# Attention on one core: the shift products of two heads as 32-row tiles, and the products with v in runs over four blocks of keys

## The chip, the cores and the metric

The kernel runs on one core of one Trainium2 chip. Its time is the device time of one launch in microseconds (us); shown are medians over runs of the same program. Besides those runs there is one profiled execution, from which all views of the trace come.

## The reference, cut to what matters

The input is x of shape (8, 1024, 512) in float32. With `xn = layernorm(x)` the result is `x + attention(xn) + ffn(xn)`.

Attention has 16 heads of 32 columns:

```python
qkv = xn @ W_attn + b_attn            # (8, 1024, 1536), split into q, k, v
att = einsum('bhqd,bhkd->bhqk', q, k) * 32 ** -0.5
att = where(causal, att, -inf)
att = softmax(att, axis=-1)
y   = einsum('bhqk,bhkd->bhqd', att, v)
out = y @ W_proj + b_proj
```

The feed-forward part quantises its input, its three weight matrices and its hidden values in blocks of 16 to a four-bit grid, and computes `down(silu(gate(xn)) * up(xn))` with 1408 hidden columns. The change does not touch it, but its products share TensorE with attention.

## The kernel before

**Work units.** Tokens are handled in 64 tiles of 128. Attention is cut into 64 units, one for each of the 8 batches and each pair of heads (`HU = 2`). A unit goes through two passes. The first, `maxima` (L555), computes the scores with queries on the partitions (product L594), takes each row's maximum on VectorE (L608) and the sum of its exponentials on ScalarE (L566). It leaves, for every query and head, the negated maximum as two float32r parts, a high and a low one, and the inverse of the sum. The second, `weigh` (L668), computes the scores again with keys on the partitions, and is what the change edits.

**The second pass.** A unit's queries come in two halves `Q` of 512 columns (`W`). For each half the loop over `j` (L704) runs over the blocks of 128 keys that the half may look at: four for the first half, eight for the second. In the half's own four blocks the columns before the block's first query are left out (`q0`), so products there are 512, 384, 256 and 128 columns wide; elsewhere they are 512 wide. For each block and each of the two heads there are two products into one PSUM bank:

- the **shift product** (L710) puts the negated maximum of each query into all 128 partitions. Its moving operand is `shT`, a tile of 128 rows in which four strips of 32 rows belong to the four pairs of half and head; only the first two rows of a strip hold anything (the high and the low part), and the others are zero. Its stationary operand `pick[:, k, :]` has ones in the 32 rows of strip `k` and zeros elsewhere, so that all 128 rows are run through though one strip counts;
- the **score product** (L713) adds keys times queries. Its 128 rows are the four combinations of high and low parts of q and k, 32 rows each.

Both are float32r and stand in the trace as one matmul record each. ScalarE then writes the exponential into an SBUF tile `pr` (L721; a pool of eight buffers), and for the blocks on the diagonal GpSimd clears the triangle (L727). The **products with v** (`weighted`, L688 to L701) take these tiles: stationary are 32 columns of `vs`, moving is `pr`, and the 32 output rows go to one of four strips of the bank `y`, by head and by whether the block is even or odd; `tile_position=(0, row)` names that strip, so that four such products can run in TensorE at once, each in 32 columns of the array. They are float32, which the trace shows as two matmul records for each product. Before the change, two blocks (four products) are done in one run.

**What sets the order.** The order of the instructions on every engine is written by the program itself. Each part of the work is a generator that yields the estimated cost of what it has just emitted, the time on the plan's clock before which it should not go on, and the number of PSUM banks that it wants. `merge` (L994) picks whose turn it is, among six streams: `weigh`, `maxima`, the feed-forward network, the quantisation, the preparation of later tiles, and `finish`. So numbers such as the `cost` in L722 are planned costs; they decide what is emitted between what, and nothing else. Loads and stores go out on SyncE's queue at planned times (`Later`). All products but those with v use the six shared banks of `Banks` (L185); `y` and the accumulator of the down projection `acc` (L793) have a bank each.

Other lines that the text speaks of: L349 transposes, L464 and L509 the projections to q, k and v, L641 the transpose of the maxima, L815 the gate and up products and L793 the down product of the network, L920 the output projection.

Of the kernel before, what the change touches and what calls it, by code (L numbers as in the profile page):

```python
# [27 lines left out]
def kernel(  # L28
# [35 lines left out]
    HD = D // HEADS  # L64
# [6 lines left out]
    HU = 2  # L71
    NU = HEADS // HU
    assert NU == NT
    QG = 4
    W = QG * P
# [38 lines left out]
    pick = const.tile([P, HPC, P], F32R, name="pick")  # L114
# [33 lines left out]
    def act(columns, after=0.0, function="other"):  # L148
        if function == "other":
            function = table[0]  # L150
        switch = TABLE if function != table[0] else 0.0
        table[0] = function
        return on("act", 0.17 + 0.00083 * columns + switch, after)
# [4 lines left out]
    def pool(us, after=0.0):  # L158
        return on("pool", us, after)
# [52 lines left out]
    banks = Banks()  # L212
# [320 lines left out]
    def load_half(un, h):  # L533
        f, r0 = un.u * HU // HPC, un.u * HU % HPC
        for name, pool, s, pieces, lst in (("qs", p5, 0, (0, 0, 1, 1), un.qs), ("ks", p6, 1, (0, 1, 0, 1), un.ks)):
            tl = pool.tile([P, HU, W], F32R, name=name)
            for g, piece in enumerate(pieces):
                nc.sync.dma_start(
                    out=tl.bitcast(F32)[g * HD : (g + 1) * HD],
                    in_=un.batch.qk[s, piece, f, r0 * HD : (r0 + HU) * HD, h * W : (h + 1) * W].rearrange(  # L540
                        "(r d) t -> d r t", d=HD
                    ),
                )
            lst.append(tl)

    def load_values(un):
        for h in range(2):
            v = p4.tile([P, QG, HU * HD], F32, name="vs")
            cols = slice(un.u * HU * HD, (un.u + 1) * HU * HD)
            nc.sync.dma_start(  # L550
                out=v, in_=un.batch.v[h * QG : (h + 1) * QG, :, cols].rearrange("t p e -> p t e")
            )
            un.vs.append(v)
# [114 lines left out]
    def weigh(un):  # L668
        f, r0 = un.u * HU // HPC, un.u * HU % HPC
        emptied = 0.0  # L670
        while un.shT is None:
            yield 0.0, clock[0] + 0.5, 0
        units_begun[0] = un.n

        def loads(Q):
            if un.n + 2 < N:
                load_half(units[un.n + 2], Q)
            if un.n + 1 < N and Q == 0:
                load_values(units[un.n + 1])

        yield 0.0, un.ready, 2

        for Q in range(2):
            Later(1.0, lambda Q=Q: loads(Q))
            y = ps_a.tile([P, W], F32, name="y")
            last = (Q + 1) * QG - 1
            waiting = []
            def weighted():  # L688
                for j, r, pr, q0 in waiting:
                    h, jj = j // QG, j % QG  # L690
                    row = (j % 2 * HU + r) * HD
                    nc.tensor.matmul(  # L692
                        y[row : row + HD, q0:],
                        lhsT=un.vs[h][:, jj, r * HD : (r + 1) * HD],
                        rhs=pr[:, q0:],
                        start=(j < 2),
                        stop=(j >= last - 1),
                        skip_group_check=True,
                        tile_position=(0, row),
                    )  # L700
                return 0.3 + (W - min(q0 for _, _, _, q0 in waiting)) * 0.0017  # L701

            ready = 0.0
            for j in range(last + 1):  # L704
                h, jj = j // QG, j % QG
                q0 = jj * P if h == Q else 0
                fresh = []
                for r in range(HU):
                    bank, w = banks.take()
                    nc.tensor.matmul(  # L710
                        w[:, q0:], lhsT=pick[:, Q * HU + r, :], rhs=un.shT[:, q0:], start=True, stop=False
                    )
                    nc.tensor.matmul(  # L713
                        w[:, q0:],
                        lhsT=un.ks[h][:, r, jj * P : (jj + 1) * P],
                        rhs=un.qs[Q][:, r, q0:],
                        start=False,
                        stop=True,
                    )
                    pr = p8.tile([P, W], F32, name="pr")  # L720
                    nc.scalar.activation(pr[:, q0:], w[:, q0:], AF.Exp)  # L721
                    cost = max(0.22, (W - q0) * 0.00089)  # L722
                    end = act(W - q0, clock[0] + cost * (r + 1), "exp")
                    banks.back(bank, end)
                    if h == Q:

                        nc.gpsimd.affine_select(  # L727
                            out=pr[:, q0 : q0 + P],
                            in_=pr[:, q0 : q0 + P],
                            compare_op=ALU.is_ge,  # L730
                            fill=0.0,
                            base=0,
                            pattern=[[1, P]],
                            channel_multiplier=-1,
                        )
                        end = pool(0.37, end)
                    if j == 1 and q0 > 0:

                        nc.gpsimd.memset(pr[:, :q0], 0.0)
                        end = pool(0.2)  # L740
                    fresh.append((j, r, pr, 0 if j < 2 else q0))
                if j % 2 == 0 and waiting:
                    yield 2 * cost, max(ready, emptied), 0
                    yield weighted(), 0.0, 2
                    waiting = []
                else:
                    yield 2 * cost, 0.0, 2 if j < last else 0
                waiting += fresh
                ready = end
            yield 0.0, max(ready, emptied), 0  # L750
            cost = weighted()
            yu = p1.tile([P, W], F32, name="yu")
            nc.scalar.copy(yu, y)
            emptied = act(W, clock[0] + cost)

            def store(Q=Q, yu=yu):
                rows = slice(r0 * HD, (r0 + HU) * HD)
                for part in range(2):
                    nc.sync.dma_start(
                        out=un.batch.y[part, f, rows, Q * W : (Q + 1) * W],  # L760
                        in_=yu[part * HU * HD : (part + 1) * HU * HD, :],
                    )
                un.batch.units_done += Q

            Later(emptied - clock[0] + 0.5, store)
            yield cost, 0.0, 2
# [275 lines left out]
    with tc.manual_schedule(  # L1042
# [10 lines left out]
        for k in range(2 * NC):  # L1053
            w = p8.tile([P, NC, P], F32, name="pr")
# [9 lines left out]
        for col in range(2 * D, 3 * D, 2 * P):  # L1064
            w = p2.tile([P, NC, 2 * P], F32, name="wa")
# [48 lines left out]
        def preparations():  # L1114
            for n in range(AHEAD, N, QT):
# [3 lines left out]
        merge(  # L1119
            [  # L1120
                Stream((weigh(un), 17.5, un.n, 1.0) for un in units),
                Stream((maxima(un), 6.0, un.n - 1 - SOONER, 1.0) for un in units[1:]),
                Stream(networks()),
# [43 lines left out]
```

## Time and profile before

| what | value |
|---|---|
| median of 3 runs (lowest, highest) | 4314.11 us (4312.82, 4318.57) |
| the profiled execution's own time | 4316.67 us |
| its span, first to last instruction | 4315.0 us |
| mean granted TensorE clock | 0.990 of full speed |
| ScalarE busy | 2331.1 us (54%) |
| VectorE busy | 2946.8 us (68%) |
| GpSimd busy | 551.6 us (13%) |
| shift products L710, 1536 records | 643.7 us busy, mean 427 ns |
| score products L713, 1536 records | 519.4 us busy, mean 346 ns |
| products with v L692, 3072 records | 358.1 us busy, mean 509 ns |

In the profile PE is TensorE's matmuls and PEld its weight loads, DVE is VectorE, ACT ScalarE, POOL GpSimd and SP SyncE. A matmul's recorded end is modelled, and matmuls of one group overlap in the record; the time that a product takes on TensorE is therefore read from the starts of neighbours, not from its own duration. The time outside the span is 4316.67 - 4315.0 = 1.67 us.

### The profile page before, as it was taken

How to read it: one execution, taken by the hardware profiler on the slowest of the kernel's cores; microseconds unless marked ns; L12 is line 12 of the kernel's file. 1: busy time of each engine (PE TensorE's matmuls, PEld its weight loads, DVE VectorE, ACT ScalarE, POOL GpSimd, SP SyncE). 2: the span in 40 equal slices, each digit the busy share in tenths (PEclk: the TensorE clock that was granted, in tenths of full speed). 3: DMA queues.
4: the chain of work that ended last, by engine and by line, in shares of the span. 5: the costliest groups of instructions: out<-in, count | busy, mean ns of one | idle time of the engine just before them, and what ended most of it. 6: DMA issues, size and time to landing. Idle time of an engine off the chain costs nothing.

```text
span 4315.0 us, 58501 instructions
## 1 busy us (share of the span) xinstructions
PE 4186.5 (97%) x17684; PEld 2574.7 (60%) x17684; DVE 2946.8 (68%) x6811; ACT 2331.1 (54%) x5918; POOL 551.6 (13%) x1295
## 2 busy tenths in 40 slices
PE   7779999999999999999999999999999999999998
PEld 6655556566666666666666666666666555555555
DVE  6786666666666766666766666766666677777755
ACT  2246565655555555555555555555555566666640
POOL 0001111111111111111111111111111111111110
PEclk9889999999999999999999999999999999999999
DMA  5654343454545554555554555554554433433424
GB/s 183 176 165 118 106 118 111 125 153 139 148 141 144 153 159 139 149 140 145 152 159 137 150 140 143 154 160 135 152 138 125 120 84 91 102 85 94 103 57 124
DMA packets 564185, 573.83 MB, mean 133 GB/s; under 512 B 114976, under 2 KB 420128, under 8 KB 563872
## 3 DMA queue, kind: packets, MB, share of 16 engines
q1 hardware_dynamic: 563872, 570.10, 47.8%
q8 instruction: 142, 2.33, 0.2%
q14 instruction: 171, 1.40, 0.1%
HBM read 400.56 MB, written 169.35 MB: 132 GB/s over the span
## 4 chain that ended last, share of the span: by engine, by line
PE 83%; DMA 3%; ACT 2%; DVE 2%; issue 1%; SPq 1%; ACTq 0%; POOL 0%; DVEq 0%
PE bank L815 26%; PE acc L793 13%; PE y L692 7%; PE bank L464 7%; PE bank L710 7%; PE bank L713 6%; PE bank L594 5%; PE bank L920 5%; PE bank L509 4%; PE bank L349 2%; ACT bank L566 2%; DVE neg L608 1%; DMA yT<-y_kept 1%; DMA ks<-y_kept 1%; DMA vs<-v_kept 0%
## 5 line engine op out<-in xcount | busy, mean ns | idle before, releaser
L608 DVE TENSOR_REDUCE neg<-bank 128x1 f32<-128x512 f32 (+3 forms) x1280 | 805.6, 635 | 292.3 <-PE bank L594 265.7
L721 ACT ACTIVATE pr<-bank 128x512 f32<-128x512 f32 (+3 forms) x1536 | 666.9, 494 | 517.5 <-PE bank L713 508.5
L566 ACT ACTIVATE bank<-bank,neg 128x512 f32<-128x512 f32 (+3 forms) x1536 | 857.9, 560 | 113.5 <-DVE neg L608 101.5
L727 POOL TENSOR_SCALAR_AFFINE_SELECT pr<-pr 128x128 f32<-128x128 f32 x1024 | 395.3, 397 | 3145.9 <-ACT pr L721 3139.2
L815 PE MATMUL bank<-wuT,xqT 128*128 128x512 f32 (+1 forms) x1536 | 674.7, 564 | 9.0 <-ACT bank L566 6.5
L815 PE MATMUL bank<-wgT,xqT 128*128 128x512 f32 (+1 forms) x1536 | 671.5, 561 | 0.0
L793 PE MATMUL acc<-wdT,hqT 128*128 128x512 f32 x1408 | 662.9, 595 | 1.3 <-ACT hqT L350 1.3
L594 PE MATMUL bank<-ks,qs 128*128 128x512 f32 (+3 forms) x1536 | 631.1, 469 | 20.1 <-ACT bank L566 14.5
L710 PE MATMUL bank<-shT,pick 128*128 128x512 f32 (+3 forms) x1536 | 643.7, 427 | 5.2 <-DMA shT<-shift_kept 3.6
L713 PE MATMUL bank<-qs,ks 128*128 128x512 f32 (+3 forms) x1536 | 519.4, 346 | 0.0
L606 DVE TENSOR_TENSOR bank<-bank,mask 128x128 f32<-128x128 f32 (+1 forms) x768 | 259.5, 338 | 342.6 <-PE bank L594 253.8
L594 PEld LDWEIGHTS bank<-ks,qs 128*128 128x128 f32 x1536 | 273.2, 191 | 266.4 <-issue 132.6
L476 ACT ACTIVATE full<-bank,bqk 128x256 f32<-128x256 f32 x256 | 107.5, 471 | 572.0 <-PE bank L464 503.6
L710 PEld LDWEIGHTS bank<-shT,pick 128*128 128x128 f32 x1536 | 290.8, 189 | 201.0 <-issue 94.1
L815 PEld LDWEIGHTS bank<-wuT,xqT 128*128 128x128 f32 x1536 | 273.8, 190 | 218.3 <-issue 140.6
L815 PEld LDWEIGHTS bank<-wgT,xqT 128*128 128x128 f32 x1536 | 276.0, 190 | 213.0 <-issue 164.8
L793 PEld LDWEIGHTS acc<-wdT,hqT 128*128 128x128 f32 x1408 | 258.3, 190 | 224.4 <-issue 204.1
L692 PE MATMUL y<-pr,vs 128*32 128x512 f32 (+3 forms) x3072 | 358.1, 509 | 4.7 <-POOL pr L727 4.6
L464 PE MATMUL bank<-xnT,wa 128*128 128x256 f32 x1536 | 352.2, 383 | 0.5 <-ACT xnT L350 0.5
L713 PEld LDWEIGHTS bank<-qs,ks 128*128 128x128 f32 x1536 | 291.2, 190 | 84.4 <-issue 51.9
L464 PEld LDWEIGHTS bank<-xnT,wa 128*128 128x128 f32 x1536 | 292.2, 192 | 64.8 <-issue 27.5
L566 ACT ACTIVATION_READ_ACCUMULATOR bank<-bank,neg 128x1 f32 x1536 | 316.0, 206 | 0.0
(97 smaller groups left out, 4501.5 us busy)
## 6 DMA issues: line engine op xcount, KB each, us to landing
wa<-in_L_attn_W_attn_dram SPq DMA_DIRECT2D x146, 512.0 KB
qs<-qk_kept SPq DMA_DIRECT2D x512, 128.0 KB
ks<-qk_kept SPq DMA_DIRECT2D x512, 128.0 KB
wp<-in_L_attn_W_proj_dram SPq DMA_DIRECT2D x81, 512.0 KB
qk_kept<-high SPq DMA_DIRECT2D x128, 256.0 KB
qk_kept<-full SPq DMA_DIRECT2D x128, 256.0 KB
y_kept<-yu SPq DMA_DIRECT2D x256, 128.0 KB
yT<-y_kept SPq DMA_DIRECT2D x112, 256.0 KB
```

Of the source, the lines that this page charges most:

```text
L464: nc.tensor.matmul(pq[:, j, :], lhsT=halves[j][:, c, :], rhs=xnT[:, c, :], start=(c == 0), stop=(c == NC - 1),)
L566: nc.scalar.activation(part, part, AF.Exp, bias=neg[:, kind, k + j : k + j + 1], accum_out=sums[:, kind, k + j : k + j + 1],)
L594: nc.tensor.matmul(sc[:, j * n : (j + 1) * n], lhsT=un.qs[Q][:, r, i * P : (i + 1) * P], rhs=un.ks[h][:, r, :n], start=True, stop=True,)
L606: nc.vector.tensor_tensor(corner, corner, mask.unsqueeze(1).broadcast_to([P, count, P]), ALU.add)
L608: nc.vector.tensor_reduce(neg[:, kind, k : k + count], each, AX.X, ALU.max, negate=True)
L692: nc.tensor.matmul(y[row : row + HD, q0:], lhsT=un.vs[h][:, jj, r * HD : (r + 1) * HD], rhs=pr[:, q0:], start=(j < 2), stop=(j >= last - 1 ...
L710: nc.tensor.matmul(w[:, q0:], lhsT=pick[:, Q * HU + r, :], rhs=un.shT[:, q0:], start=True, stop=False)
L713: nc.tensor.matmul(w[:, q0:], lhsT=un.ks[h][:, r, jj * P : (jj + 1) * P], rhs=un.qs[Q][:, r, q0:], start=False, stop=True,)
L721: nc.scalar.activation(pr[:, q0:], w[:, q0:], AF.Exp)
L727: nc.gpsimd.affine_select(out=pr[:, q0 : q0 + P], in_=pr[:, q0 : q0 + P], compare_op=ALU.is_ge, fill=0.0, base=0, pattern=[[1, P]], channe ...
L793: nc.tensor.matmul(tl.acc, lhsT=job.hqT[:, j, :], rhs=wdT[:, i, :], start=(i == 0), stop=(i == NI - 1))
L815: nc.tensor.matmul(job.g, lhsT=job.tl.xqT[:, c, :], rhs=wT[:, c, job.i0 : job.i0 + job.w], start=(c == 0), stop=(c == NC - 1),)
```

## The change

The edit is confined to `weigh`.

1. For each block of keys, two PSUM banks are taken together. The two shift products (one for each head) are emitted one after the other, each from the 32 rows of its own strip alone, with `tile_position=(k * 32, 0)`, so that they stand in two different strips of 32 rows of TensorE's array. The two score products follow, each with its exponential; before, the order was shift, score, shift, score.
2. The products with v are emitted once for every four blocks (eight products, after the fourth block's exponentials) where it was once for every two blocks, after the next block's products.
3. The planned costs change: for the products of one head and block from `max(0.22, columns * 0.00089)` to `max(0.2, 0.05 + columns * 0.00067)`, and for a run of products with v to 0.3 plus the sum over its pairs of blocks.

```diff
-                return 0.3 + (W - min(q0 for _, _, _, q0 in waiting)) * 0.0017
+                return 0.3 + sum(W - q0 for _, _, _, q0 in waiting[:: 2 * HU]) * 0.0017
 
             ready = 0.0
             for j in range(last + 1):
                 h, jj = j // QG, j % QG
                 q0 = jj * P if h == Q else 0
                 fresh = []
-                for r in range(HU):
-                    bank, w = banks.take()
+                held = [banks.take() for _ in range(HU)]
+                for r, (_, w) in enumerate(held):
+                    k = Q * HU + r
+                    quarter = slice(k * HD, (k + 1) * HD)
                     nc.tensor.matmul(
-                        w[:, q0:], lhsT=pick[:, Q * HU + r, :], rhs=un.shT[:, q0:], start=True, stop=False
+                        w[:, q0:],
+                        lhsT=pick[quarter, k, :],
+                        rhs=un.shT[quarter, q0:],
+                        start=True,
+                        stop=False,
+                        tile_position=(k * HD, 0),
                     )
+                for r, (bank, w) in enumerate(held):
                     nc.tensor.matmul(
                         w[:, q0:],
                         lhsT=un.ks[h][:, r, jj * P : (jj + 1) * P],
...
-                    cost = max(0.22, (W - q0) * 0.00089)
+                    cost = max(0.2, 0.05 + (W - q0) * 0.00067)
...
-                if j % 2 == 0 and waiting:
+                waiting += fresh
+                ready = end
+                if j % QG < QG - 1:
+                    yield 2 * cost, 0.0, 2
+                elif j < last:
                     yield 2 * cost, max(ready, emptied), 0
                     yield weighted(), 0.0, 2
                     waiting = []
                 else:
-                    yield 2 * cost, 0.0, 2 if j < last else 0
-                waiting += fresh
-                ready = end
+                    yield 2 * cost, 0.0, 0
```

## The prediction, on record before the changed kernel ran

> **What bounds the kernel now.** I read the page's first part, then the busy time by stretches of the span, then the waits, and last the timeline of TensorE in a short window. From the page:
>
> ```profile
> span 4315.0 us, 58501 instructions
> PE 4186.5 (97%) x17684; PEld 2574.7 (60%) x17684; DVE 2946.8 (68%) x6811; ACT 2331.1 (54%) x5918; POOL 551.6 (13%) x1295
> ```
>
> TensorE is busy for 97%, no other engine for more than 68%. By stretches (columns: span, then busy time and records of PE, PEld, DVE, ACT, POOL, clock, DMA share, GB/s):
>
> ```profile
> 500.00:4100.00 3600.00, 3576.66 (x15109) 2155.30 (x15109) 2463.34 (x5714) 2068.43 (x5259) 491.62 (x1146) 1.00 0.49 133
> ```
>
> In the 3600 us that hold most of the attention units TensorE is idle for 23 us and its clock is full. A busy matmul record proves little, so I ask whether TensorE waits for data:
>
> ```profile
> PE bank L594 <- ACT bank L566: 14.5, 45, 2.9
> PE bank L815 <- ACT bank L566: 6.5, 19, 0.4
> PE y L692 <- POOL pr L727: 4.6, 2, 3.4
> PE bank L710 <- ACT bank L566: 1.1, 3, 0.6
> ```
>
> It does not (total us, times, longest): neither banks nor finished exponentials hold it back for more than a few us in all. So the end is set by the order of TensorE's own instructions, and what the change adds to or takes from that order moves the end one for one. Everything below is counted there.
>
> **What a change of tile costs.** The trace has no 32-row product. It has the nearest thing, the products with v in 32 columns of the array, between full ones. TensorE's matmuls (start, duration):
>
> ```profile
> 2017.35 0.39 PE L710 MATMUL bank<-shT,pick 128*128 128x512 f32 x1
> 2017.58 0.40 PE L713 MATMUL bank<-qs,ks 128*128 128x512 f32 x1
> 2017.91 1.06 PE L692 MATMUL y<-pr,vs 128*32 128x512 f32 x8
> 2018.90 0.50 PE L710 MATMUL bank<-shT,pick 128*128 128x512 f32 x1
> 2019.24 0.40 PE L713 MATMUL bank<-qs,ks 128*128 128x512 f32 x1
> 2019.48 0.40 PE L710 MATMUL bank<-shT,pick 128*128 128x512 f32 x1
> ```
>
> and the weight loads of the same stretch:
>
> ```profile
> 2017.36 0.19 PEld L713 LDWEIGHTS bank<-qs,ks 128*128 128x128 f32 x1
> 2017.91 0.16 PEld L692 LDWEIGHTS y<-pr,vs 128*32 128x32 f32 x8 [0.36 <-PE bank L713]
> 2018.90 0.19 PEld L710 LDWEIGHTS bank<-shT,pick 128*128 128x128 f32 x1 [0.84 <-issue]
> 2019.01 0.19 PEld L713 LDWEIGHTS bank<-qs,ks 128*128 128x128 f32 x1
> ```
>
> Among full tiles a product of 512 columns takes 0.23 us (2017.35 to 2017.58, 2019.24 to 2019.48), and its weights were loaded beside the product ahead (L713's load at 2017.36). A float32 pass of 512 columns takes 0.428 us (median between neighbours of L815). The first L692 comes 0.33 us after L713, not 0.23: **0.10 us of emptying**. Its four products overlap, so the eight records are two passes, 0.86 us. The next load, of L710, starts at 2018.90, about 0.09 us after the last pass has run in: emptying again. It was not fetched ahead, so L710 starts to stream only when the load is through at 2019.01: **0.11 us of open load**. From L713 at 2017.58 to L713 at 2019.24 are 1.66 us, of which 0.23 + 0.86 + 0.23 = 1.32 us are products: **one run in and out costs 0.34 us**. L641, with 48 columns but no tile position, has no such gap ahead or behind (0.43 and 0.11 us to its neighbours' loads, their own time).
>
> **The change part by part.**
>
> *Shift products.* A half needs one pair for each block: 12 pairs in a unit, six of 512 columns and two each of 384, 256 and 128, so over 64 units 384 + 128 + 128 + 128 = 768 pairs. Median time between starts: 0.231, 0.175, 0.118 and 0.112 us; at 128 it is the weight load, not the columns, that sets it. In L692 four products start within 0.02 us of each other in different columns; I take it that two in different rows do so too. Saved, for the three wider forms: 384 x 0.231 + 128 x (0.175 + 0.118) = **126.2 us**.
>
> *Changes of tile.* The changed order has full, 32-row, full at every pair. With the price of the column tiles: 0.094 emptying (0.522 - 0.428 between records of L815 and L692), 0.107 load of 128 columns with nothing to hide it, and both again on the way out, as a full score product always follows: 0.402 us. For 640 pairs **+257.3 us**. At 128 columns: before 4 x 0.112 = 0.448; after 0.094 + 0.107 + 0.06 + 0.094 + 0.107 + 0.112 = 0.574 us; 128 x 0.126 = **+16.1 us**. In 83 of the 768 pairs the changed order puts a product with v just ahead, so one way out and one way in fall together: 83 x 0.201 = **-16.7 us**.
>
> *Runs with v.* 384 runs of two blocks become 192 of four; the passes stay. 192 x 0.34 = **-65.3 us**.
>
> *The rest.* ScalarE, VectorE, GpSimd and the DMA queues get the same instructions; only their order moves with the planned costs. Two banks taken at once: the second of six is held about 0.23 us longer; the waits for banks above (14.5 + 6.5 + 1.1) might double, so 0 to +22 us; I take 0, since the exponential behind it takes 0.59 us and ScalarE is half idle. A run now waits for four blocks' exponentials, and behind it on TensorE stand all other streams. At the end of a half this was so before, and cost 4.6 us; new are 64 runs, after block 3 of the second half, which wait for ScalarE alone: 0 to +10 us, taken as 0. The eight buffers of `pr` are all held by a run; the next exponential needs one, but its products stand behind the run on TensorE anyway: 0. Replanning can move waits either way; TensorE's 23 idle us in the middle say how much a better order could gain, and I allow 20 us both ways.
>
> Sum: -126.2 + 257.3 + 16.1 - 16.7 - 65.3 = **+65.2 us**. On the profiled execution's 4316.67 us that gives 4381.9; that execution is 2.56 us above the median, so against the median of 4314.11 I forecast **4380 us**.
>
> **What is unknown, from both sides.** No row shows a change to 32 rows. Lower end: it costs nothing, as between L815, L710 and L641. Upper end: the price above, with the second strip's load queued behind the first (768 x 0.107 = +82 us). I take the price of the column tiles because it is the only row with a tile position. The change gains as long as one pair costs less than about (126.2 + 65.3) / 768 = 0.25 us for going in and out; my price is 0.40.
>
> The Trainium skill, "TensorEngine Tiling (Array Packing)", Tiling Modes, Key Properties, says that changing the tiling mode, not just the tile, drains TensorE, and its list of modes has 32x128 apart from 128x128. The 0.10 and 0.09 us gaps around L692 agree for columns; no run here yet shows rows. By that rule the sum stays at 4380. Against it stands "TensorE: Matmul & The Clock Gate", Part 2 (Step-by-step) and Part 3 (The mechanism): weight loads are pulled ahead when row groups differ or the load goes to the background buffer, and row tiles use no further bus. If that held across a change of tile, the sum would be that of rival 2 below, 4235. The load at 2018.90, not fetched ahead, shows that it does not hold for columns.
>
> **The rivals.**
>
> 1. *No price for rows* (the other side). If what makes TensorE empty is particular to 32-column tiles, a pair costs three products: -126.2 - 65.3 and 0 to -14 at 128 columns, -192 to -206 us: **4110 to 4123**. For it: L641 and the changes between float32 and float32r cost nothing. Against: the only rows with a tile position pay.
> 2. *Emptying, but loads hidden.* 640 x 0.188 = 120.3, merged places -83 x 0.094 = -7.8, at 128 columns about 0: -126.2 + 120.3 - 7.8 - 65.3 = -79 us: **4235**. With half of a price more or less: 4170 to 4305. For it: a load of 0.107 us would fit under a product of 0.23. Against: 2018.90.
> 3. *Second load queued*: +65.2 + 82 = +147 us: **4461**. For it: full loads follow each other 0.11 us apart (2018.90, 2019.01). Against: L692's eight loads take 0.16 us together.
> 4. *The two products do not run side by side*, so the change doesn't do what it says: 65.2 + 126.2 + 128 x 0.06 = +199 us: **4513**. Against: L692's four do.
>
> **How the numbers follow.** My case (one price as for columns, loads of the two strips together): 0.40, by itself 4345 to 4415, which is the replanning and a drain of half the size on the way out (768 x 0.047 = 36 us). Rival 3: 0.12. Rival 4: 0.03. Rival 2: 0.27. Rival 1: 0.14. Near the break-even price: 0.04. So slower 0.55, within 0.2% (8.6 us, about what a measurement of this kernel can tell from no change) 0.04, faster 0.41. The range leaves out rivals 1 and 4, 0.17 together: **4165 to 4470 us**.
>
> **What would show it.** In the timeline around a pair: the first score product's load. If it starts about 0.09 us after the shift products have run in, and the next 0.11 us later, my price is right; if it lies beside the shift products, rival 2; if the first score product also starts 0.23 us after the shift products, rival 1. The two shift products should start within 0.02 us (not 0.11: rival 3; not 0.23 or more: rival 4). Runs with v should be 16 records with 0.34 us beyond their four passes. The waits of TensorE for ScalarE and GpSimd should stay under 50 us; if they grow past that, the order failed and not the tile.

## The result and the profile after

The changed kernel takes 4440.49 us (median of 4 runs, 4436.65 to 4441.36) against 4314.2 us: ratio 1.0287, 95% interval 1.0271 to 1.0304. It is 126 us slower where 65 us were forecast. Its profiled execution took 4440.41 us, 123.7 us more than that of before.

The first part of the changed kernel's profile, and its stretch of 3700 us that answers to the one shown of before:

```profile
span 4438.7 us, 58758 instructions
PE 4298.1 (97%) x17684; PEld 2480.0 (56%) x17684; DVE 2957.2 (67%) x6811; ACT 2332.7 (53%) x5918; POOL 529.2 (12%) x1295
```

```profile
500.00:4200.00 3700.00, 3654.21 (x15002) 2057.08 (x15000) 2468.75 (x5690) 2056.08 (x5224) 466.33 (x1136) 1.00 0.47 129
```

The number of matmul records is the same and TensorE is as full as it was; the added time is TensorE's. But its idle time in the middle has doubled, from 23 us of 3600 to 46 us of 3700. Of its waits, the four lines that answer to those shown of before (total us, times, longest):

```profile
PE bank L594 <- ACT bank L566: 35.5, 103, 2.9
PE bank L825 <- ACT bank L566: 5.5, 19, 0.3
PE y L692 <- POOL pr L735: 1.9, 1, 1.9
PE bank L712 <- ACT bank L566: 0.7, 2, 0.5
```

The scores of `maxima` (L594) wait for banks 103 times, where it was 45 times. Over the whole list, the waits of TensorE for ScalarE and GpSimd add up to 63.5 us, where it was 47.4.

The timeline of TensorE around one pair of shift products of 512 columns (start, duration), and the weight loads of the same stretch:

```profile
2028.28 0.50 PE L712 MATMUL bank<-shT,pick 32*128 32x512 f32 x2
2028.71 0.73 PE L721 MATMUL bank<-qs,ks 128*128 128x512 f32 x2
2029.27 0.59 PE L803 MATMUL acc<-wdT,hqT 128*128 128x512 f32 x1
```

```profile
2028.28 0.18 PEld L712 LDWEIGHTS bank<-shT,pick 32*128 32x128 f32 x2 [0.56 <-DVE step L326]
2028.70 0.30 PEld L721 LDWEIGHTS bank<-qs,ks 128*128 128x128 f32 x2 [0.25 <-issue]
2029.04 0.42 PEld L803 LDWEIGHTS acc<-wdT,hqT 128*128 128x128 f32 x2
```

Both shift products, loads included, are in one group: the second starts 3 ns after the first (median over all pairs). The load of the first score product comes 0.43 us after the start of theirs, though the shift products need only 0.231 us: 0.107 for their own open load, 0.231, and 0.09 of emptying. From the first score product's start to the network's are 2029.27 - 2028.71 = 0.56 us for two products that need 0.46: its own open load again. Medians over the trace; the sums are within 0.01 us of the forecast, but for the pairs of 128 columns, which take 0.05 us more:

| columns | emptying, way in | to the first score | to the second | to what follows | sum | forecast | full rows |
|---|---|---|---|---|---|---|---|
| 512 | 0.094 | 0.429 | 0.336 | 0.231 | 1.090 | 1.095 | 0.924 |
| 384 | 0.094 | 0.370 | 0.281 | 0.175 | 0.920 | 0.927 | 0.700 |
| 256 | 0.094 | 0.313 | 0.223 | 0.118 | 0.748 | 0.756 | 0.472 |
| 128 | 0.094 | 0.255 | 0.164 | 0.111 | 0.624 | 0.574 | 0.448 |

**Where the rest went.** I divided TensorE's time into two parts. Its *own work* is, for each record, the time that its columns or its open load take, plus every emptying: a sum of prices, read from medians, times their counts. What is left between the starts of neighbours is *waiting*, also where it is too short for the profile's list. Only both parts together are measured directly. (Of the waiting some 100 us lie in the first and last 300 us of each kernel. Some 21 us of each execution lie ahead of TensorE's first start or behind its last.)

| kernel | own work, us | waiting, us | profiled execution, us |
|---|---|---|---|
| before | 4101.4 | 194.1 | 4316.67 |
| changed | 4181.3 | 238.1 | 4440.41 |

So 80 us are own work (the forecast had 65) and 44 us are waiting (the forecast had 0 within 20). Divided in another way, each start against the end of the columns ahead of it, they are 76 and 48 us; the division is good to some 5 us here, and to 10 in `e2_rows_only` below. The theory to be tested: the change of tile costs 0.40 us a pair whatever else is done, and the 44 us come from the order of the instructions, not from the tiles. Rivals: the runs of four blocks wait by themselves; or the price of a pair is less, and order makes up the loss.

### The profile page after: what moved, and what is told of

It is laid out like the page before. It is cut to its first block, busy times and chain, and to the rows that moved or that the text cites. A ratio compares the mean times of both kernels' runs of the same rounds, so it can differ in the third digit from the quotient of the medians.

```text
span 4438.7 us, 58758 instructions
## 1 busy us (share of the span) xinstructions
PE 4298.1 (97%) x17684; PEld 2480.0 (56%) x17684; DVE 2957.2 (67%) x6811; ACT 2332.7 (53%) x5918; POOL 529.2 (12%) x1295
## 4 chain that ended last, share of the span: by engine, by line
PE 85%; DVE 5%; ACT 4%; issue 1%; DMA 1%; SPq 0%; ACTq 0%; POOL 0%; DVEq 0%; POOLq 0%
PE bank L825 26%; PE acc L803 12%; PE bank L721 9%; PE bank L464 7%; PE y L692 7%; PE bank L712 6%; PE bank L594 5%; PE bank L930 4%; PE bank L509 4%; ACT bank L566 3%; PE bank L349 2%; DVE neg L608 1%; ACT pr L729 1%; DMA shT<-shift_kept 0%; DVE scale L333 0%
## 5 line engine op out<-in xcount | busy, mean ns | idle before, releaser
L735 POOL TENSOR_SCALAR_AFFINE_SELECT pr<-pr 128x128 f32<-128x128 f32 x1024 | 375.3, 379 | 3314.7 <-ACT pr L729 3305.5
L594 PE MATMUL bank<-ks,qs 128*128 128x512 f32 (+3 forms) x1536 | 630.2, 478 | 39.8 <-ACT bank L566 35.5
L825 PE MATMUL bank<-wgT,xqT 128*128 128x512 f32 (+1 forms) x1536 | 661.3, 560 | 1.5 <-ACT pr L729 0.2
L721 PE MATMUL bank<-qs,ks 128*128 128x512 f32 (+3 forms) x1536 | 482.1, 395 | 0.0
L594 PEld LDWEIGHTS bank<-ks,qs 128*128 128x128 f32 x1536 | 274.3, 191 | 257.8 <-issue 104.5
L712 PEld LDWEIGHTS bank<-shT,pick 32*128 32x128 f32 x1536 | 144.8, 181 | 383.7 <-issue 178.3
L712 PE MATMUL bank<-shT,pick 32*128 32x512 f32 (+3 forms) x1536 | 344.7, 438 | 6.2 <-DMA shT<-shift_kept 5.3
L692 PE MATMUL y<-pr,vs 128*32 128x512 f32 (+3 forms) x3072 | 316.8, 502 | 1.9 <-POOL pr L735 1.9
L721 PEld LDWEIGHTS bank<-qs,ks 128*128 128x128 f32 x1536 | 229.0, 188 | 143.8 <-issue 118.1
## 6 DMA issues: line engine op xcount, KB each, us to landing
qk_kept<-high SPq DMA_DIRECT2D x128, 256.0 KB
qk_kept<-full SPq DMA_DIRECT2D x128, 256.0 KB
yT<-y_kept SPq DMA_DIRECT2D x112, 256.0 KB
```

The lines of the kernel that those rows point to most:

```text
L594: nc.tensor.matmul(sc[:, j * n : (j + 1) * n], lhsT=un.qs[Q][:, r, i * P : (i + 1) * P], rhs=un.ks[h][:, r, :n], start=True, stop=True,)
L692: nc.tensor.matmul(y[row : row + HD, q0:], lhsT=un.vs[h][:, jj, r * HD : (r + 1) * HD], rhs=pr[:, q0:], start=(j < 2), stop=(j >= last - 1 ...
L712: nc.tensor.matmul(w[:, q0:], lhsT=pick[quarter, k, :], rhs=un.shT[quarter, q0:], start=True, stop=False, tile_position=(k * HD, 0),)
L721: nc.tensor.matmul(w[:, q0:], lhsT=un.ks[h][:, r, jj * P : (jj + 1) * P], rhs=un.qs[Q][:, r, q0:], start=False, stop=True,)
L735: nc.gpsimd.affine_select(out=pr[:, q0 : q0 + P], in_=pr[:, q0 : q0 + P], compare_op=ALU.is_ge, fill=0.0, base=0, pattern=[[1, P]], channe ...
L825: nc.tensor.matmul(job.g, lhsT=job.tl.xqT[:, c, :], rhs=wT[:, c, job.i0 : job.i0 + job.w], start=(c == 0), stop=(c == NC - 1),)
```

## The experiments

### One edit at a time

`e1_runs_only`: the kernel before with the new `weighted` and the new grouping of the yields, no 32-row tiles, the old pair costs.

> Only the second edit: products with v in runs over four blocks; shift products over all 128 rows in the old order (shift, score, shift, score) with the old planned costs. My theory (192 runs fewer at 0.34 us, nothing else): 4314 - 65 = 4249 us, within 20 us, and TensorE's waits for banks stay near those of before. Rival (the waits that the changed kernel shows beyond the prediction, about 45 us, come from runs that need four blocks' exponentials and all eight buffers of pr): 4314 - 65 + 45 = 4294 us, with the waits of the scores L594 for banks doubled.

Measured 4299.78 us, ratio 0.996 (0.9945 to 0.9975). My theory's 4249 us was missed by 51 us, the rival's 4294 by 6. Own work is 4036.3, 65.1 us less than before; but that is the price of a run times 192, so the price has to be read from the trace itself:

```profile
2060.23 1.92 PE L692 MATMUL y<-pr,vs 128*32 128x512 f32 x16
2062.09 0.51 PE L594 MATMUL bank<-ks,qs 128*128 128x512 f32 x1
2062.43 1.45 PE L817 MATMUL bank<-wgT,xqT 128*128 128x384 f32 x4
```

A run of 16 records of 512 columns takes 1.854 us to the next start (median; 1.86 here), where two runs of eight take 2 x 0.996 in the kernel before: 0.138 us saved inside, and with them one emptying ahead (0.094) and one open load behind (0.107), together 0.339 us for each of 192 runs. The forecast had 0.34. Waiting is 242.6 us, 48 us more, and the scores of `maxima` wait as the rival said:

```profile
PE bank L594 <- ACT bank L566: 30.5, 95, 3.1
```

The rival's size was right: in this order the runs of four come with the waits.

`e2_rows_only`: the changed kernel with `weighted` and the yields of before.

> Only the first edit with its planned costs: shift products as 32-row tiles, two heads side by side; products with v in runs over two blocks as before. The order has 165 places with a product with v just ahead of a pair. My theory (0.402 us for in and out of every pair): 4314 + 150 - 165 x 0.201 = 4431 us without waits from replanning, up to 4475 with those that the changed kernel has. Rival (the price of a pair is small and the loss comes from the runs of four): 4250 to 4330 us.

Measured 4452.9 us, ratio 1.0318 (1.0303 to 1.0333). The time lies inside my 4431 to 4475 us, far outside the rival's 4250 to 4330. Own work 4236.1 (+134.7), waiting 194.9, as before; divided in the other way, +124 and +11 us. So the 32-row tiles, the two banks taken at once and their planned costs bring hardly any wait; the loss is TensorE's own work. It is 8 to 18 us over my 117 us, according to the division, and what these are is open: the pairs of 128 columns are in the 117 with their measured 0.624 us.

`e3_full_rows_same_order`: the changed kernel without its tile.

```diff
                     nc.tensor.matmul(
                         w[:, q0:],
-                        lhsT=pick[quarter, k, :],
-                        rhs=un.shT[quarter, q0:],
+                        lhsT=pick[:, k, :],
+                        rhs=un.shT[:, q0:],
                         start=True,
                         stop=False,
-                        tile_position=(k * HD, 0),
                     )
```

> The changed kernel with one thing undone: the shift products run over all 128 rows, without a tile position. The order of all instructions on TensorE is that of the changed kernel. My theory (the tile itself costs 150 us less 17 us where it follows a product with v): 4440 - 133 = 4307 us, that is about the time before, as 65 us saved by the longer runs are nearly eaten by waits that the new order brings. Rival (the tile costs half of that, and the rest of the loss is order and waits): 4370 us.

Measured 4330.83 us, ratio 1.0035 (1.0022 to 1.0048). With the order of every engine kept, the tile alone is worth 4440.5 - 4330.8 = 110 us (the two profiled executions differ by 115). Own work differs by 4181.3 - 4036.8 = 144.5 us; waiting is 267.2 here and 238.1 with the tiles; I take this to be ScalarE getting more time beside a slower TensorE, which no run shows by itself. My 133 lies between the two. The time expected was 4307 us, 24 less than measured; the rival's 4370 is 39 more, and its price (half of mine, 66 us) is out.

### The price of a change of tile

`e5_rows_one_by_one`: the kernel before, each shift product alone as a 32-row tile.

```diff
                     bank, w = banks.take()
+                    k = Q * HU + r
+                    quarter = slice(k * HD, (k + 1) * HD)
                     nc.tensor.matmul(
-                        w[:, q0:], lhsT=pick[:, Q * HU + r, :], rhs=un.shT[:, q0:], start=True, stop=False
+                        w[:, q0:],
+                        lhsT=pick[quarter, k, :],
+                        rhs=un.shT[quarter, q0:],
+                        start=True,
+                        stop=False,
+                        tile_position=(k * HD, 0),
                     )
```

> The kernel before with its order and planned costs, but every shift product alone as a 32-row tile (shift, score, shift, score): twice as many changes of tile and nothing side by side. My theory (0.402 us for every way in and out, one by one): at 512, 384 and 256 columns 0.804 us for a pair, at 128 columns about 0.58, so 640 x 0.804 + 128 x 0.58 - 121 x 0.201 = 565 us: 4315 + 565 = 4880 us, less up to 30 us of waits that the slower TensorE covers. Rival (the price belongs to the pair, to two tiles at work at once or to two banks written at once, and not to the change of tile): 4315 to 4450 us.

Measured 4862.91 us, ratio 1.1263 (1.124 to 1.1286): inside the 4850 to 4880 us of my theory, far over the rival's 4450. The timeline shows the plainest form of the price, one product after each change:

```profile
2300.02 0.38 PE L712 MATMUL bank<-shT,pick 32*128 32x256 f32 x1
2300.33 0.38 PE L720 MATMUL bank<-qs,ks 128*128 128x256 f32 x1
2300.64 0.38 PE L712 MATMUL bank<-shT,pick 32*128 32x256 f32 x1
2300.95 0.38 PE L720 MATMUL bank<-qs,ks 128*128 128x256 f32 x1
2301.26 1.06 PE L692 MATMUL y<-pr,vs 128*32 128x512 f32 x8
```

Each of the four takes 0.31 us where 0.118 are needed: 0.094 and 0.107 on top, in and out alike. The price belongs to the change, not to two tiles at work at once.

`e9_rows_two_blocks`: the shift products of two blocks between one way in and one way out.

```diff
-            for j in range(last + 1):
+            for j0 in range(0, last + 1, 2):
+                held = []
+                for j in (j0, j0 + 1):
+                    q0 = j % QG * P if j // QG == Q else 0
+                    for r in range(HU):
+                        held.append((j, r, q0, *banks.take()))
+                for j, r, q0, _, w in held:
...
+                spent = 0.4
+                for j, r, q0, bank, w in held:
...
+                    spent += max(0.16, (W - q0) * 0.00068)
+                    end = act(W - q0, clock[0] + spent, "exp")
...
+                if j % QG < QG - 1:
+                    yield spent, 0.0, 4
```

> The changed kernel with the shift products of two blocks (four products, four banks) between one way in and one way out of the 32-row tiles, then the four score products; runs with v over four blocks as changed; planned costs set to this. Half as many changes of tile. My theory (0.402 us for in and out, whatever lies between): two blocks of 512 columns take 0.402 + 6 x 0.231 = 1.79 us where full rows take 1.85; 512 with 384: 1.62, as full rows; 256 with 128: about 1.09 against 0.92. In all 128 x (-0.06 + 0 + 0.17) = +14 us against full rows, -26 us for 129 places just behind a product with v, -65 us for the longer runs: 4316 - 77 = 4239 us without new waits; four of six banks held at once may bring 0 to 50 us of waits, so 4239 to 4290 us. Rival (the price goes with the products, not with the changes): 4400 to 4440 us.

Measured 4401.34 us, ratio 1.0189 (1.0174 to 1.0204): 111 us over the range of my theory, and inside the rival's 4400 to 4440. By the total alone the rival would have won; the trace decides against it. Medians for two blocks, way in included: 1.80, 1.62 and 0.98 us (1.79, 1.62 and 1.09 expected), so the price goes with the changes. What I had too small are the waits with four banks of six held:

```profile
2086.44 0.38 PE L713 MATMUL bank<-shT,pick 32*128 32x256 f32 x1 [0.25 <-ACT full L476]
2087.11 0.80 PE L713 MATMUL bank<-shT,pick 32*128 32x256 f32 x2 [0.29 <-ACT bank L566]
2088.26 0.32 PE L713 MATMUL bank<-shT,pick 32*128 32x128 f32 x1 [0.36 <-ACT bank L566]
```

```profile
PE y L692 <- POOL pr L738: 27.3, 16, 1.9
PE bank L594 <- ACT bank L566: 19.6, 54, 3.1
PE bank L713 <- ACT bank L566: 18.6, 59, 0.7
```

The shift products of one group stop between each other for the next bank, with TensorE already changed over. Summed over the 384 groups, the mean time exceeds the median by 94 us, and the runs with v are 46 us longer than in the changed kernel, as they wait for the last triangle: 140 of the 162 us by which the total exceeds 4239. No run holds the four banks apart from the plan that comes with them. The total therefore doesn't say what fewer changes are worth; the groups' medians do.

### The waits

`e4_measured_costs`: the changed kernel with the planned cost of a pair as the trace shows it.

```diff
-                    cost = max(0.2, 0.05 + (W - q0) * 0.00067)
+                    cost = 0.235 + (W - q0) * 0.0006
```

> The changed kernel with the planned cost of one head and block set to what the trace shows for a pair (0.235 + 0.0006 for each column, so 1.08 us for a pair of 512 columns where the change plans 0.79); the computation is the same, only the order moves. It puts 28 pairs behind a product with v, not 83, which costs 11 us. Theory of the planned costs (the plan gives weigh too little time, finishes it early in its interval and leaves the scores of maxima in clumps that wait for banks): 4440 - 45 + 11 = 4406 us, and the waits of L594 for ScalarE fall back from 35 us to under 20. Rival (the waits come from the runs of four or the pairs of banks): 4440 to 4451 us.

Measured 4410.51 us, ratio 1.0217 (1.0201 to 1.0232). Waiting 196.2 us, as before the change, with runs of four and pairs of banks still there; L594 waits for ScalarE 16.3 us. My theory had 4406 us and under 20; the rival's 4440 to 4451 is out. So neither makes TensorE wait by itself; the order does.

If planned numbers alone decide, a planned number should mend the runs of four without tiles too. `e6`, `e7`, `e10`, `e11` are `e1` with another length for `weigh`'s stream; `e8` is the control, the kernel before with 15.8.

```diff
-                Stream((weigh(un), 17.5, un.n, 1.0) for un in units),
+                Stream((weigh(un), 14.8, un.n, 1.0) for un in units),
```

> The second edit alone, as in e1, with one planned number changed: the length that weigh's stream is said to have, 17.5 before, set to 16.4, so that a unit's work (planned costs sum to about 13.9 after the longer runs, 14.8 before) is again spread over the same share of its interval as before. Theory of the pacing (runs of four save their 65 us on TensorE, and lose 48 to waits only because the plan finishes a unit's weigh too early and leaves the scores of maxima in clumps): 4316 - 65 = 4251 us, waits of L594 for ScalarE under 20 us. Rival (the waits are those of runs of four themselves): 4300 us as in e1.

> As e6, with 14.8, so that a unit's weigh is spread over nearly its whole interval, as it is in e4. Theory of the pacing: 4235 to 4255 us. Rival: 4300 us.

> Control: the kernel before with only weigh's planned length set from 17.5 to 15.8, which spreads its work over the same share as in e7. If pacing only restores what the longer runs disturb, 4310 to 4320 us, as before; if it takes waits away in any kernel, 4290 us, and the comparison of e6 and e7 has to be made against this one.

> As e7 (longer runs alone), with the planned length 14.0. TensorE's own work is that of e1, e6 and e7. If a shorter planned length keeps the scores of maxima apart from each other, 4240 to 4265 us as in e7; if the order answers to such numbers without a rule, anything from 4250 to 4320 us.

> As e7, with the planned length 15.6, between e7 (14.8: 4263 us) and e6 (16.4: 4316 us). If there is a rule, 4263 to 4316 us and in proportion about 4290 us; if there is none, outside of it as well.

The last column counts, in the order of TensorE's instructions, how many of the 1536 first-pass scores (L594) stand directly behind another one.

| kernel | planned length | median us | ratio (95%) | own work | waiting | score behind score |
|---|---|---|---|---|---|---|
| before | 17.5 | 4314.2 | 1 | 4101.4 | 194.1 | 626 |
| e8, before | 15.8 | 4346.55 | 1.0068 (1.0053 to 1.0083) | 4101.1 | 223.8 | 583 |
| e1, runs of four | 17.5 | 4299.78 | 0.996 (0.9945 to 0.9975) | 4036.3 | 242.6 | 751 |
| e6, runs of four | 16.4 | 4315.64 | 0.9997 (0.9987 to 1.0006) | 4036.0 | 256.0 | 734 |
| e11, runs of four | 15.6 | 4298.26 | 0.995 (0.9934 to 0.9967) | 4039.1 | 237.2 | 702 |
| e7, runs of four | 14.8 | 4262.64 | 0.9873 (0.9858 to 0.9887) | 4041.0 | 202.0 | 638 |
| e10, runs of four | 14.0 | 4284.52 | 0.9919 (0.9904 to 0.9934) | 4036.3 | 223.1 | 616 |

e7 is the fastest, 1.3% ahead of the kernel before and 4.0% ahead of the changed one. My theory of pacing has fallen as a rule: e6 restores the share of before and is the worst of the five with runs of four, the steps are not in proportion, and the control, brought to the same share as e7, loses 0.7%. The ranges that the theory gave to e6, e7 and e10 were all missed (e7's by 8 us), and so were both that the control had; e11 lies inside its own, but not in proportion. What stands is narrower: the five kernels with runs of four have the same products in the same runs (own work the same to 5 us), so the 53 us between them is order, and runs of four need not wait (e7: 202 us).

Most of the added waits of the changed kernel can be seen where the scores stand together. TensorE in the changed kernel, then ScalarE in the same stretch:

```profile
2052.20 1.42 PE L594 MATMUL bank<-ks,qs 128*128 128x512 f32 x5
2054.18 0.50 PE L594 MATMUL bank<-ks,qs 128*128 128x512 f32 x1 [0.56 <-ACT bank L566]
2054.85 0.50 PE L594 MATMUL bank<-ks,qs 128*128 128x512 f32 x1 [0.17 <-ACT bank L566]
2055.52 0.50 PE L594 MATMUL bank<-ks,qs 128*128 128x512 f32 x1 [0.17 <-ACT bank L566]
2056.08 1.13 PE L509 MATMUL bank<-wa,xnT 128*128 128x256 f32 x4
```

```profile
2054.03 0.65 ACT L566 ACTIVATE bank<-bank,neg 128x512 f32<-128x512 f32 x1
2054.60 0.20 ACT L566 ACTIVATION_READ_ACCUMULATOR bank<-bank,neg 128x1 f32 x1
2054.69 0.66 ACT L566 ACTIVATE bank<-bank,neg 128x512 f32<-128x512 f32 x1
2055.26 0.21 ACT L566 ACTIVATION_READ_ACCUMULATOR bank<-bank,neg 128x1 f32 x1
```

Eight scores follow each other with nothing between. The first five fill the banks; from then on each comes 0.67 us after the last, ScalarE's pace for an exponential and the read of its sum (0.66 us), where a score of 512 columns needs 0.23 of TensorE. Each costs 0.44 us, of which the profile's list shows 0.17, because a matmul's record reaches beyond its columns. In the first-pass scores directly behind another one, waiting is 41 us before, 73 in the changed kernel, 63 in e1, 75 in e6, 77 in e11, and 35 to 46 in e2, e4, e7, e8 and e10, where fewer than 650 stand so. That is 32 of the 44 us that the changed kernel waits more than before, and 22 of the 48 of e1; the rest is spread over other lines. Nor is the count all: e8 has the fewest but one and waits 25 us more than before at the transposes.

## Why the prediction was right, and where it was not

- **The total: right in direction, half of it in size, and inside the range by the room left for a rival.** The 4440 us lie 25 us above the 4345 to 4415 us that my own case was given. The range reached to 4470 for rival 3 (4461), and rival 3 is out, as the next points show; that the measured time lies near its total is chance.
- **TensorE is the bound: right.** The time between its first and its last start grew by 123.9 us (79.9 by own work, 44.0 by waiting); the profiled executions differ by 123.7. The further step, that nothing but its own products sets the end, held for the tiles and the runs and not for the 44 us.
- **The price of a change to 32 rows, taken from the 32-column tiles: right.** 0.094 and 0.107 us each way, in the changed kernel, in e5 at twice the count, in e9 at half of it; e3 shows what they cost in time, 110 us. With the medians the pairs cost 384 x 0.166 + 128 x (0.220 + 0.276 + 0.176) = 150 us, forecast 257.3 - 126.2 + 16.1 = 147.2. Rivals 1 and 2 are out: the price is there, and the loads are not hidden.
- **The two products side by side: right.** 3 ns apart, loads too; rivals 3 and 4 are out.
- **At 128 columns: 0.05 us a pair too little**, 6 us in all. I had not charged the second score's load (0.107 us), which is longer than its columns. With them the own work should have grown by 72 us; the other 4 to 8 us are within what the division can tell.
- **Runs with v, -65.3: right**, 192 x 0.339 = 65.1 us by the trace of e1.
- **What failed is the term "replanning", taken as 0 within 20 us.** It is +44 us of waiting in the changed kernel and +48 in e1. The step behind it was wrong too: from 23 idle us in the middle I concluded what an order could gain, and said nothing of what it could lose. The order of before was not a neutral one: the control e8 shows 30 us from one planned number. And the profile's list of waits was no measure of it, since it counts 0.17 of each 0.44 us. So I had read "it does not wait" where the starts show 194 us. The sign that I had named for a failed order, more than 50 us of waits for ScalarE and GpSimd, was badly placed: the list had 47.4 us before and 63.5 after, and its "the order failed and not the tile" does not hold, as the tile cost 110 us besides.
- **The costs taken as nothing** (two banks at once, a run that needs four blocks): right in themselves. e2 has the first and no new wait; e4 and e7 have the second and hardly one. Waits came only where I let four banks be held, in e9.

On the Trainium skill: "TensorEngine Tiling (Array Packing)", Key Properties, says that a change of tiling mode drains TensorE; the 0.094 us around 32-row products agree. The pull-ahead of weight loads in "TensorE: Matmul & The Clock Gate", Part 2 and Part 3, holds here among tiles of one mode (in e9 the third shift product's load is hidden behind the first's columns: the product starts 0.335 us after the first, about 0.107 + 0.231) and not across a change.

**What stays open:** which feature of the plan makes a good order. Five lengths gave no rule. Why the runs of four bring waits at 17.5 and hardly any at 14.8 is not shown. That clumps of first-pass scores wait for ScalarE is seen in the trace; an order made by hand without them was not tried.

## What to carry to other kernels

A change of tile shape on TensorE costs about 0.2 us each way here (emptying and an open weight load), so packing pays only if what lies between two changes saves more than 0.4 us: two 32-row products of 512 columns save 0.23. Where one engine is nearly full and its order is made by a plan, split its time into own work and waiting from the starts of its records, and judge an edit by the first, with prices read from medians; a single planned number moved the waiting by 5 to 42 us (e4, e6 to e8, e10, e11). Then tune the order for the edit that lowers the own work: here the longer runs alone, worth 65 us, of which the first order kept 17 and a better one 54.

## What the runs showed of the hardware that was not expected

- The third and fourth 32-row products of a group start right behind the first two in the same strips (0.335 us after them, about 0.107 + 0.231, their loads from 0.107 us on): the load for a strip at work is hidden, and the price is for the change of shape alone.
- A product of 48 columns without a tile position (L641) causes no emptying, one of 32 columns with a position does.
- A wait of 0.44 us can stand in the profile as 0.17: a matmul's recorded end lies about 0.27 us behind the end of its columns (0.50 us recorded for 0.23).
